# One gathered tile in 88 fetched row by row by SyncE, and segment tables fetched with one transfer a run: a graph network on one Trainium2 core

## The chip, the cores and the metric

The kernel runs on one core of one Trainium2 chip. The metric is device time in microseconds (us). The engines are named as in the profile: PE (TensorE; PEld is its weight load), DVE (VectorE), ACT (ScalarE), POOL (GpSimd) and SP (SyncE). SP computes nothing here: it issues DMAs, each with the register work for its addresses. In the profile's rows, SPq, DVEq and POOLq are the sequencers of these engines.

## The reference, cut to what matters

A graph has N = 6250 nodes with 128 numbers each and 200000 edges (src, dst), sorted by dst; an edge has 4 numbers of its own. Two convolutions and one attention run over the edges.

```python
def mesh_conv(x, src, dst, ea, w1, b1, g, bt, w2, b2):
    m = concatenate([x[dst], x[src], ea]) @ w1 + b1
    m = silu(group_norm(m, g, bt)) @ w2 + b2
    return segment_sum(m, dst) / clip(count(dst), 1)

h = silu(group_norm(mesh_conv(relu(layernorm(x)), ...))) + time_embedding
h = silu(group_norm(mesh_conv(h, ...))) + relu(layernorm(x))
q, k, v = (h @ w + b for each of three)
logits = (q[dst] * k[src]).sum(-1) * scale + (ea @ ew + eb)      # 8 heads
pe = exp(logits - segment_max(logits, dst)[dst])
o = segment_sum(pe / segment_sum(pe, dst)[dst] * v[src], dst) @ ow + ob
return x + h + group_norm(o)
```

The product with w1 is taken per node, not per edge: before each stage a table of x[dst]'s part (`a_d`) and one of x[src]'s part (`b_d`, in attention `kv_d`, 256 wide) lie in HBM, and what remains per edge is to fetch a row of each and add or multiply them.

## The kernel before

**Tiles.** The edges lie in 1563 tiles of 128, eight tiles to a chunk (TPC), 196 chunks (NCH). Three stages go over all chunks, one after another: conv 1, conv 2, attention. `pipeline` (L755) emits a stage; step n of its loop works on several chunks at once, and `in_order` (L743) pins the emitted order on DVE, SP, ACT and PE. So an instruction that waits holds all that is emitted behind it on its engine. A conv step emits:

- `fetch(n+2)`: SP loads the chunk's first row number into a register (`value`, L618) and fetches 112 rows of `a_d` into one of three buffers (`pk`, L647); for every second chunk it fetches the comparison tile `ohT` of two chunks (`load_group`: L631, 896 KB, and L634, 40 KB; two buffers). POOL gathers x[src]'s part: eight indirect DMAs, one a tile, 128 rows each (`gather`, L661), into one of four buffers g (in attention one of eleven).
- `products(n+1)`: PE multiplies pk and ohT to m (L1089, 8 products; in attention qe, L1294).
- `compared(n+2)`: ACT turns ohT into a one-hot matrix (L656, L657).
- `second`: for a chunk some steps back, DVE builds the one-hot `oh` (L667), norms h (L1111, L1114, L1115), ACT takes silu (L1116), PE sums by node (u, L1121), ACT and DVE put it into the node table.
- `first(n)`: DVE adds m and g into h (L1096), which frees the buffer of g; ACT squares it (L1098).
- `early`, `batch`, `aside`, `reduce`: a one-hot ahead of time, node work of finished windows, in conv 1 the preparation of tables for attention (`deferred`), and the variance (L1100).

The g buffer of a chunk comes free by L1096 of the chunk four before; POOL then gathers the next one or more chunks in one go. POOL's order isn't pinned, but POOL does hardly anything else.

**The attention's tables.** The maximum per segment is scanned over runs of up to eight chunks with two tables of marks, `nbs_d` and `nbe_d`. Both lie in HBM as one row of 128 per tile. A run needs them as [8 chunks x 8 heads, 1024], each chunk's row repeated for the eight heads, so `load_runs` (L1317) issues one DMA of 16 KB a chunk and table (L1323), which reads the row eight times: 392 in the stage, up to 16 in a row. `in_rows` (L468) writes these tables in conv 1, as part of `deferred`.

**Names of the waits.** "POOL g L661 <- DVE h L1096" is POOL's wait for a free buffer of g. "SPq L631 <- remote" and "SPq L647 <- remote" are SP's waits ahead of the fetches of ohT and pk, for a buffer that is still in use.

Of the kernel before, what the change touches and what calls it, by code (L numbers as in the profile page):

```python
# [8 lines left out]
FP = mybir.dt.float32  # L9
BF = mybir.dt.bfloat16  # L10
I32 = mybir.dt.int32
AF = mybir.ActivationFunctionType
# [3 lines left out]
SP = mybir.EngineType.SP  # L16
# [5 lines left out]
P = 128  # L22
D = 128
H = 8
# [3 lines left out]
TPC = 8  # L28
EPC = TPC * P
# [3 lines left out]
LG = 2  # L33
WN = 112
SOON = 24
TAILS = [7, 7, 6, 5, 4, 3, 4]
BY_ACT = 60
KE = 5
KW = WN + KE
DB = D + H  # L40
# [2 lines left out]
KV = 2 * D  # L43
EPS = 1e-5
BIG = 1e30
# [4 lines left out]
def kernel(ctx: ExitStack, tc: tile.TileContext, x, src, dst, eat, w, out):  # L50
# [9 lines left out]
    nc = tc.nc  # L60
    N = x.shape[0]
    EI = src.shape[1]
    NCH = -(-EI // TPC)
    EW = NCH * TPC
# [6 lines left out]
    dram = ctx.enter_context(tc.tile_pool(name="dram", bufs=1, space=DRAM))  # L71
# [8 lines left out]
    def by_chunk(t):  # L80
        return t.rearrange("p (c t) -> p c t", t=TPC)
# [8 lines left out]
    ident = const.tile([P, P], FP, name="ident")  # L90
# [53 lines left out]
    b_d = {i: dram.tile([NW * P, D], FP, name=f"b_d{i}") for i in (1, 2)}  # L144
    kv_d = dram.tile([NW * P, KV], FP, name="kv_d")
# [2 lines left out]
    dwl_d = dram.tile([P, EW], FP, name="dwl_d")  # L148
    dmod_d = dram.tile([P, EW], FP, name="dmod_d")
    rel_d = dram.tile([EW, P], FP, name="rel_d")  # L150
    nbs_d = dram.tile([EW, P], BF, name="nbs_d")
    nbe_d = dram.tile([EW, P], BF, name="nbe_d")

    dm0 = const.tile([P, EW], BF, name="dm0")
    ef = const.tile([P, EW], BF, name="ef")
# [39 lines left out]
    with tc.tile_pool(name="node0", bufs=1) as np_, tc.tile_pool(name="prep", bufs=1) as pp, \  # L195
# [8 lines left out]
        step = 8  # L204
# [38 lines left out]
        for a in range(0, NW, 4):  # L243
            m = min(4, NW - a)
# [12 lines left out]
            tp = pst.tile([P, 4, P], FP, name="tp")  # L257
# [96 lines left out]
    def steps_of(i):  # L354


        ends, due, n = {}, {}, 0
        for m in spread(i):
            ends[n + m] = list(range(n, n + m))
            due.setdefault(n + m + (n < NCH - (sum(TAILS) if i == 3 else SOON)), []).extend(ends[n + m])  # L360
            n += m
        waiting, todo, left = [], [], NCH
        while left:
            n = len(todo)
            waiting += due.get(n, ())
# [26 lines left out]
    def deferred(dp, ps):  # L392
# [56 lines left out]
        def bank():  # L449
            return ps.tile([P, 4, P], FP, name="nd", tag="nd")  # L450
# [16 lines left out]

        def in_rows(t, d_):  # L468

            for k in range(0, EW, 4 * P):  # L470
                yield from to_rows(t, d_, -BIG, bank(), dp.tile([P, 4, P], BF, name="sbd"), k, nc.sync)

        kept = []

# [147 lines left out]
    class Chunk:  # L622
        oh = None

    def load_group(c, pools):

        n = min(LG, NCH - c)
        m = min(n * TPC, EI - c * TPC)
        t = pools["ohT"].tile([P, LG, EPC], FP, name="ohT")
        f = t.rearrange("p c e -> p (c e)")  # L630
        nc.sync.dma_start(  # L631
            out=f[:WN, :m * P],
            in_=rel_d[c * TPC:c * TPC + m, :].rearrange("t p -> (t p)")[None, :].to_broadcast([WN, m * P]))
        nc.sync.dma_start(out=f[WN:KW, :m * P], in_=eat[:, c * EPC:c * EPC + m * P])  # L634
        pools[c // LG] = t
# [20 lines left out]
        nc.scalar.activation(k.ohT[:WN, :], k.ohT[:WN, :], AF.Square, bias=minus_p[:WN])  # L656
        nc.scalar.activation(k.ohT[:WN, :], k.ohT[:WN, :], AF.Relu, bias=1.0, scale=-4.0)  # L657

    def gather(k, g, table_d):
        for t in range(k.nt):  # L660
            nc.gpsimd.indirect_dma_start(  # L661
                out=g[:, t, :table_d.shape[1]], out_offset=None, in_=table_d,
                in_offset=bass.IndirectOffsetOnAxis(ap=k.src[:, t:t + 1], axis=0))
# [91 lines left out]
    def pipeline(i, stage, aside=iter(())):  # L755

        start = len(nc.cur_bb.bb.instructions)
        ends, todo = steps_of(i)
        starts = {n: j for j, (n, _) in enumerate(plans[i])}
        ahead = stage.ahead
        ks, under_way, said = {}, [], {}
        for c in range(ahead):
            ks[c] = stage.fetch(c)
            compared(ks[c])
        stage.products(ks[0])  # L770
        for n, seconds in enumerate(todo):
            if n + ahead < NCH:
                ks[n + ahead] = stage.fetch(n + ahead)
            if n + 1 < NCH and stage.soon:
                stage.products(ks[n + 1])
            run = [ks[c] for c in ends.get(n, ())]
            stage.root(run)
            if n + ahead < NCH and stage.soon:
                compared(ks[n + ahead])
            first = (lambda k: lambda: stage.first(k))(ks[n]) if n < NCH else None  # L780
            if stage.second(run, [ks.pop(c) for c in seconds], first) and first:
                first()
            stage.finish()
            if n + ahead < NCH and not stage.soon:
                compared(ks[n + ahead])
            if n + 1 < NCH and not stage.soon:
                stage.products(ks[n + 1])
            if n < NCH:
                stage.early(ks, n, todo[n + 1])
            if n in starts:  # L790
                for _ in aside:
                    pass
                under_way.append(stage.batch(starts[n]))
            for g in list(under_way):
                if said.get(g) == "held" and n + 1 in ends:
# [257 lines left out]
    def conv(i):  # L1053
# [4 lines left out]
        with ExitStack() as es:  # L1058
# [15 lines left out]
                nc.vector.tensor_copy(t, s)  # L1074
            np_, nd = pool("np", 1), pool("nd", 1, space=PSUM)
            nodes = Nodes(np_of(np_, "A", "o"), lambda: nd.tile([P, BN, D], FP, name="nd", tag="nd"))
            side = es.enter_context(ExitStack())
            aside = iter(())
            if i == 1:
# [53 lines left out]
            class Stage:  # L1133
                ahead, soon = 2, True
                sums, late, roots, next = [], [], False, 0
                var, j, sd = None, 0, None

                def fetch(self, c):
                    k = loads(c, pools, a_d[i], self.ahead)
                    k.g = gp.tile([P, TPC, D], FP, name="g")  # L1140
                    gather(k, k.g, b_d[i])
                    k.h = hs[c % len(hs)]
                    return k

# [68 lines left out]
                    add_late(self.sums[0])  # L1213

            stage = Stage()
            nodes.var = lambda: stage.var[:, NV:]
            pipeline(i, stage, aside)
            side.close()
# [43 lines left out]
    with ExitStack() as es:  # L1262
# [17 lines left out]
        def bank():  # L1280
            return banks()[:, 0, :].rearrange("p (t e) -> p t e", e=P)
# [35 lines left out]
        def load_runs(run, bp):  # L1317

            nb = {}
            for name, d_ in (("nbs", nbs_d), ("nbe", nbe_d)):  # L1320
                nb[name] = bp.tile([G * H, EPC], BF, name=name)
                for j, c in enumerate(run):
                    nc.sync.dma_start(  # L1323
                        out=nb[name][j * H:(j + 1) * H, :],
                        in_=d_[c * TPC:(c + 1) * TPC, :].rearrange("t p -> (t p)")[None, :].to_broadcast([H, EPC]))
            return nb

        def maxima(run, lg, nb, bp):
# [92 lines left out]
        class Stage:  # L1421
# [3 lines left out]

            def __init__(self, bp):
                self.bp = bp
                self.runs = list(steps_of(3)[0].values())
                self.nb = load_runs(self.runs.pop(0), bp)

            def fetch(self, c):
                k = loads(c, pools, a_d[3], self.ahead)
                k.g = gp.tile([P, TPC, KV], FP, name="g")
                gather(k, k.g, kv_d)
                return k

            def products(self, k):
# [79 lines left out]
                merge_late(self.sums[0])  # L1517
                add_late(self.sums[0])

        with tc.tile_pool(name="bpa", bufs=1) as bp, tc.tile_pool(name="ohTa", bufs=2) as pools["ohT"]:  # L1520
            pipeline(3, Stage(bp))

        n = NW - NWD
# [87 lines left out]
```

## Time and profile before

| what | value |
|---|---|
| median of 3 runs | 8112.13 us (8091.78 to 8127.0) |
| profiled execution, its own time | 8070.85 us |
| its span in the trace | 8068.5 us |
| granted PE clock, mean | 0.679 |
| instructions in the trace | 72388 |
| DMA engines, mean rate | 99 GB/s |

A row of a group reads: line, engine, operation, output<-inputs, count | busy us, mean ns of one | idle time before them, and what ended it. A row of a timeline reads: start, duration (of all in the row, if it says x16), engine, line, operation, and in brackets the idle time before it and what ended it; "issue" means that the engine waited for nothing that the profile shows. A row of the waits reads: engine and line, what it waited for, us in total, times, the longest. A row of one line's instructions reads: operation, count, duration in ns (shortest/median/longest), first and last start.

### The profile page before, as it was taken

To read this page: it belongs to the slowest core of one execution; us is meant where nothing else is said; L and a number is where in the kernel's file an instruction comes from. 1 tells how busy PE (TensorE), PEld (TensorE's weight loads), DVE (VectorE), ACT (ScalarE), POOL (GpSimd) and SP (SyncE) were. 2 spreads that over 40 slices of the span, in tenths; PEclk is the share of its full clock that TensorE was granted. 3 is DMA by queue.
4 is the path that set the end of the run, shared out by engine and by line. 5 is a ranking of instruction groups with operands and counts; after the bars stand their busy time and mean duration, and the time that the engine had idled before them with its cause. 6 is when DMAs were issued, how large, how long until landed. Compare 5 with 4: busy or idle time off the path is not lost. (4 is left out here: it accounts for less than half of the span.)

```text
span 8068.5 us, 72388 instructions
## 1 busy us (share of the span) xinstructions
PE 3978.0 (49%) x20935; PEld 3656.4 (45%) x20936; DVE 4993.0 (62%) x7274; ACT 3483.6 (43%) x5592; POOL 4485.6 (56%) x4706
## 2 busy tenths in 40 slices
PE   4555545544544454555555544344444555455444
PEld 3444444444443444444544544244444444444434
DVE  5767776666654566666777766255665655565446
ACT  4555555555544455555555544122222222234444
POOL 5666666666543666666566654455555555555541
PEclk7666666777666666666777767566666666666666
DMA  5433333333322333333333332343444444444431
GB/s 136 106 91 94 92 101 85 93 87 90 89 78 60 92 87 87 92 87 93 101 96 96 96 85 72 104 121 111 116 115 117 119 119 117 115 115 128 115 106 51
DMA packets 413975, 797.97 MB, mean 99 GB/s; under 512 B 102179, under 2 KB 274966, under 8 KB 379509
## 3 DMA queue, kind: packets, MB, share of 16 engines
q0 software_dynamic: 175056, 410.03, 19.0%
q1 hardware_dynamic: 232868, 379.58, 16.5%
q10 hardware_dynamic: 5632, 3.50, 0.2%
q8 instruction: 173, 2.83, 0.2%
q14 instruction: 246, 2.02, 0.1%
HBM read 751.77 MB, written 40.96 MB: 98 GB/s over the span
## 5 line engine op out<-in xcount | busy, mean ns | idle before, releaser
L661 POOL DMA_INDIRECT g<-b_d,src_i x3126 | 2969.5, 950 | 1917.1 <-DVE h L1096 987.6
L661 POOL DMA_INDIRECT g<-kv_d,src_i x1563 | 1490.2, 953 | 1363.6 <-DVE cm L1408 537.0
L1121 PE MATMUL u<-h,oh 128*128 128x129 f32 (+1 forms) x6252 | 1330.0, 381 | 1735.7 <-ACT h L1116 867.0
L1121 PEld LDWEIGHTS u<-h,oh 128*128 128x128 f32 x6252 | 1193.7, 284 | 1860.4 <-issue 943.9
L1089 PE MATMUL m<-pk,ohT 117*128 117x128 f32 x6252 | 1066.8, 324 | 687.1 <-issue 632.2
L1089 PEld LDWEIGHTS m<-pk,ohT 117*128 117x128 f32 x6252 | 988.1, 239 | 745.1 <-issue 696.5
L1372 PE MATMUL us<-v,oh 128*128 128x145 f32 x3126 | 740.0, 399 | 905.1 <-issue 549.2
L1372 PEld LDWEIGHTS us<-v,oh 128*128 128x128 f32 x3126 | 653.5, 282 | 975.9 <-issue 949.1
L1096 DVE TENSOR_TENSOR h<-m,g 128x1024 f32<-128x1024 f32 x392 | 475.1, 1212 | 971.9 <-remote 898.2
L1294 PE MATMUL qe<-pk,ohT 117*128 117x136 f32 x3126 | 588.6, 354 | 431.0 <-issue 247.0
L1294 PEld LDWEIGHTS qe<-pk,ohT 117*128 117x128 f32 x3126 | 548.7, 258 | 473.3 <-issue 286.2
L656 ACT ACTIVATE ohT<-ohT,minus_p 112x1024 f32<-112x1024 f32 x588 | 670.5, 1140 | 42.2 <-DMA ohT<-rel_d 29.6
L1116 ACT ACTIVATE h<-h 128x1024 f32<-128x1024 f32 x392 | 412.8, 1053 | 596.7 <-DVE h L1115 299.4
L657 ACT ACTIVATE ohT<-ohT 112x1024 f32<-112x1024 f32 x588 | 619.7, 1054 | 18.6
L1126 ACT ACTIVATE u<-u,mask 128x129 f32<-128x129 f32 (+1 forms) x784 | 263.8, 336 | 823.7 <-remote 763.7
L1100 DVE TENSOR_REDUCE var<-sq 128x64 f32<-128x1024 f32 x392 | 475.3, 1212 | 192.6 <-ACT sq L1098 85.2
L667 DVE TENSOR_TENSOR oh<-cps,dm 128x1024 f32<-128x1024 f32 x392 | 474.7, 1211 | 89.4 <-remote 79.2
L1385 ACT ACTIVATE us<-d 128x16 f32<-128x16 f32 x196 | 36.7, 187 | 1042.9 <-DVE d L1382 729.6
L1114 DVE TENSOR_TENSOR h<-h,cps 128x1024 f32<-128x1024 f32 x392 | 477.2, 1217 | 14.6 <-DVE h L1111 1.3
L1115 DVE TENSOR_TENSOR h<-h,cps 128x1024 f32<-128x1024 f32 x392 | 477.1, 1217 | 13.5 <-DVE h L1114 0.2
L1098 ACT ACTIVATE sq<-h 128x1024 f32<-128x1024 f32 x392 | 411.3, 1049 | 168.7 <-DVE h L1096 136.3
L1111 DVE TENSOR_TENSOR h<-h,cps 128x1024 f32<-128x1024 f32 x392 | 474.3, 1210 | 0.0
(286 smaller groups left out, 4387.7 us busy)
## 6 DMA issues: line engine op xcount, KB each, us to landing
ohT<-rel_d SPq DMA_DIRECT2D x291, 896.0 KB
g<-b_d,src_i POOLq DMA_INDIRECT x3126
pk<-a_d SPq DMA_DIRECT2D x588, 56.0 KB
g<-kv_d,src_i POOLq DMA_INDIRECT x1563
ohT<-in_eat_dram SPq DMA_DIRECT2D x291, 40.0 KB
a_d<-n_o SPq DMA_DIRECT2D x28, 256.0 KB
kv_d<-n_o SPq DMA_DIRECT2D x28, 256.0 KB
n_h<-h_d SPq DMA_DIRECT2D x19, 256.0 KB
```

What stands on the lines that cost most here:

```text
L656: nc.scalar.activation(k.ohT[:WN, :], k.ohT[:WN, :], AF.Square, bias=minus_p[:WN])
L657: nc.scalar.activation(k.ohT[:WN, :], k.ohT[:WN, :], AF.Relu, bias=1.0, scale=-4.0)
L661: nc.gpsimd.indirect_dma_start(out=g[:, t, :table_d.shape[1]], out_offset=None, in_=table_d, in_offset=bass.IndirectOffsetOnAxis(ap=k.src[ ...
L667: return nc.vector.tensor_tensor(k.oh[:, :k.nt, :], iota[:, None, :].to_broadcast([P, k.nt, P]), k.dm[:, :, None].to_broadcast([P, k.nt, P ...
L1089: nc.tensor.matmul(k.m[:, t, :], lhsT=lhs[:, t * P:(t + 1) * P], rhs=rhs, start=(j == 0), stop=(j == len(terms) - 1))
L1096: nc.vector.tensor_tensor(k.mt, k.m[:, :n], k.g[:, :n], ALU.add)
L1100: return lambda: nc.vector.tensor_reduce(var[:, at:at + n * H], sq[:, :n].rearrange("p t (g c) -> p (t g) c", c=HD), AX.X, ALU.add)
L1114: nc.vector.tensor_tensor(k.mt, k.mt, over_edges(gam, k.nt), ALU.mult)
L1115: nc.vector.tensor_tensor(k.mt, k.mt, over_edges(bet, k.nt), ALU.add)
L1121: nc.tensor.matmul(k.u[:, 0, :wide], lhsT=k.oh[:, t, :], rhs=k.h[:, t, :wide], start=(t == 0), stop=(t == k.nt - 1))
L1294: nc.tensor.matmul(k.qe[:, t // TB, at:at + DB], lhsT=lhs[:, t * P:(t + 1) * P], rhs=rhs, start=(j == 0), stop=(j == len(terms) - 1))
L1372: nc.tensor.matmul(k.u[:, :wide], lhsT=k.oh[:, t, :], rhs=k.v[:, t, :wide], start=(t == 0), stop=(t == k.nt - 1))
```

## The change

In each stage 17 chunks are picked (16, 27, ... 192: every 11th, `by_rows`). For these POOL gathers seven tiles, not eight. The eighth tile's 128 rows are fetched by SP into a tile of their own (`row_g`), in the 11 steps before the chunk's own fetch is due: in each step one instruction loads 12 row numbers into registers (8 in the last step), and then 12 DMAs fetch one row each (512 bytes, in attention 1 KB). There is such work in 187 of the 196 steps of each stage, 2176 row DMAs a stage. The row numbers come from a list on one partition (`row_at`, one DMA a picked chunk). In the step before the chunk is used, behind `early`, ACT copies `row_g` into the eighth tile of g (`put`). In SP's order a step's rows stand behind its pk and ohT, and ahead of those of the next step.

Each row is three instructions on SP (a register operation, a move, the DMA); SP's program grows from 4850 to 18135 instructions as built. The DMAs use eight completion semaphores in turn, so that a row waits for the DMA eight before it.

`nbs_d` and `nbe_d` are now [196, 8, 1024], with each chunk's row written eight times over, so that `load_runs` fetches a run with one DMA a table (some 56 in place of 392). They are written by four DMAs a table as before, with eight times the bytes, from transposes that take the tiles chunk by chunk (16 transposes a table, 13 before). The order on PE, DVE and ACT is otherwise as before; on POOL 51 gathers are missing.

```diff
+ROWS = 12
...
-    nbs_d = dram.tile([EW, P], BF, name="nbs_d")
-    nbe_d = dram.tile([EW, P], BF, name="nbe_d")
+    nbs_d = dram.tile([NCH, H, EPC], BF, name="nbs_d")
+    nbe_d = dram.tile([NCH, H, EPC], BF, name="nbe_d")
...
         def in_rows(t, d_):
-            for k in range(0, EW, 4 * P):
-                yield from to_rows(t, d_, -BIG, bank(), dp.tile([P, 4, P], BF, name="sbd"), k, nc.sync)
+            for c in range(0, NCH, P):
+                n = min(P, NCH - c)
+                for a in range(0, TPC, 4):
+                    tp = bank()
+                    for j in range(4):
+                        nc.tensor.transpose(tp[:n, j, :], by_chunk(t)[:, c:c + n, a + j], ident)
+                    yield
+                    sb = dp.tile([P, 4 * P], BF, name="sbd")
+                    nc.scalar.activation(sb[:n], tp[:n].rearrange("c t p -> c (t p)"), AF.Copy, scale=-BIG)
+                    yield
+                    nc.sync.dma_start(
+                        out=d_[c:c + n, :, a * P:(a + 4) * P], in_=sb[:n, None, :].to_broadcast([n, H, 4 * P]))
+                    yield
...
+    def by_rows():
+        span, first = -(-P // ROWS), LG + 3
+        return list(range(first + span, NCH - 1, span)), span
+
+    class Rows:
+        def __init__(self, pool, table_d, width):
+            self.pool, self.table_d, self.width = pool, table_d, width
+            self.chunks, self.span = by_rows()
+            self.starts = {c - 2 - self.span: c for c in self.chunks}
+            self.now, self.got = None, {}
+            self.at = {}
+            if self.chunks:
+                self.list_of(self.chunks[0])
+
+        def list_of(self, c):
+            t = self.pool.tile([1, P], I32, name="row_at")
+            col = c * TPC + TPC - 1
+            nc.sync.dma_start(out=t, in_=src[:, col:col + 1].rearrange("p o -> o p"))
+            self.at[c] = t
+
+        def step(self, n):
+            if n in self.starts:
+                c = self.starts[n]
+                self.now = [c, 0, self.pool.tile([P, self.width], FP, name="row_g")]
+                self.got[c] = self.now[2]
+                j = self.chunks.index(c) + 1
+                if j < len(self.chunks):
+                    self.list_of(self.chunks[j])
+            if self.now:
+                c, e, t = self.now
+                m = min(ROWS, P - e)
+                _, at = nc.values_load_multi_w_load_instructions(
+                    self.at[c][0:1, e:e + m], engines=[SP], min_val=0, max_val=N - 1,
+                    skip_runtime_bounds_check_because="a source node")
+                for j, a in enumerate(at):
+                    nc.sync.dma_start(out=t[e + j:e + j + 1, :], in_=self.table_d[bass.ds(a, 1), :self.width])
+                self.now[1] = e + m
+                if e + m == P:
+                    self.now = None
+
+        def put(self, k):
+            if k.c in self.got:
+                nc.scalar.copy(k.g[:, TPC - 1, :self.width], self.got.pop(k.c))
...
-    def gather(k, g, table_d):
-        for t in range(k.nt):
+    def gather(k, g, table_d, lone=()):
+        for t in range(k.nt - bool(lone and k.c in lone)):
...
             if n + ahead < NCH:
                 ks[n + ahead] = stage.fetch(n + ahead)
+            stage.rows.step(n)
...
                 stage.early(ks, n, todo[n + 1])
+            if n + 1 < NCH:
+                stage.rows.put(ks[n + 1])
...
-                for j, c in enumerate(run):
-                    nc.sync.dma_start(
-                        out=nb[name][j * H:(j + 1) * H, :],
-                        in_=d_[c * TPC:(c + 1) * TPC, :].rearrange("t p -> (t p)")[None, :].to_broadcast([H, EPC]))
+                nc.sync.dma_start(
+                    out=nb[name][:len(run) * H, :],
+                    in_=d_[run[0]:run[-1] + 1, :, :].rearrange("c h e -> (c h) e"))
```

Conv's and attention's `fetch` hand the picked chunks to `gather`; the row tiles have a pool of two buffers.

More of the change, by code (lines that the diff above doesn't have):

```diff
@@ L1076, in conv @@
             nodes = Nodes(np_of(np_, "A", "o"), lambda: nd.tile([P, BN, D], FP, name="nd", tag="nd"))
+            rw = pool("rw", 2)
             side = es.enter_context(ExitStack())
@@ L1140, in fetch @@
                     k.g = gp.tile([P, TPC, D], FP, name="g")
-                    gather(k, k.g, b_d[i])
+                    gather(k, k.g, b_d[i], self.rows.chunks)
                     k.h = hs[c % len(hs)]
@@ L1215, in conv @@
             stage = Stage()
+            stage.rows = Rows(rw, b_d[i], D)
             nodes.var = lambda: stage.var[:, NV:]
@@ L1427, in __init__ @@
                 self.bp = bp
+                self.rows = Rows(rw, kv_d, KV)
                 self.runs = list(steps_of(3)[0].values())
@@ L1433, in fetch @@
                 k.g = gp.tile([P, TPC, KV], FP, name="g")
-                gather(k, k.g, kv_d)
+                gather(k, k.g, kv_d, self.rows.chunks)
                 return k
@@ L1518, in flush @@
                 add_late(self.sums[0])
-        with tc.tile_pool(name="bpa", bufs=1) as bp, tc.tile_pool(name="ohTa", bufs=2) as pools["ohT"]:
+        with tc.tile_pool(name="bpa", bufs=1) as bp, tc.tile_pool(name="rwa", bufs=2) as rw, \
+                tc.tile_pool(name="ohTa", bufs=2) as pools["ohT"]:
             pipeline(3, Stage(bp))
```

## The prediction

> **What bounds the kernel now.** The chain of waits that ended last is no help: it holds no share above 0% and stays in the last microseconds. So the busy times come first, then the stretches by stage, then timelines of one stretch.
>
> ```profile
> PE 3978.0 (49%) x20935; PEld 3656.4 (45%) x20936; DVE 4993.0 (62%) x7274; ACT 3483.6 (43%) x5592; POOL 4485.6 (56%) x4706
> ...
> L661 POOL DMA_INDIRECT g<-b_d,src_i x3126 | 2969.5, 950 | 1917.1 <-DVE h L1096 987.6
> ```
> ```profile
> 0.00:2572.00 2572.00, 1286.64 (x7016) 1193.73 (x7018) 1680.97 (x1925) 1317.66 (x1635) 1496.10 (x1576) 0.70 0.34 92
> 2572.00:5090.00 2518.00, 1275.26 (x6994) 1183.30 (x6994) 1657.45 (x1738) 1282.87 (x1563) 1495.84 (x1567) 0.69 0.33 91
> 5090.00:8068.00 2978.00, 1416.08 (x6929) 1279.35 (x6928) 1654.58 (x3611) 883.03 (x2395) 1493.69 (x1564) 0.65 0.40 112
> ```
>
> No engine is full, in total or in a stage (the rows are conv 1, conv 2 and attention; the columns after the length are PE, weight load, DVE, ACT, POOL, clock, DMA share, GB/s). Several queues wait for each other in turn. What the turn looks like is seen in the timeline of POOL over five chunks of conv 2.
>
> ```profile
> 3288.66 0.95 POOL L661 DMA_INDIRECT g<-b_d,src_i  x1 [4.41 <-DVE h L1096]
> 3289.91 0.95 POOL L661 DMA_INDIRECT g<-b_d,src_i  x1 [0.30 <-issue]
> ...
> 3317.42 0.95 POOL L661 DMA_INDIRECT g<-b_d,src_i  x1 [0.30 <-issue]
> 3324.15 0.95 POOL L661 DMA_INDIRECT g<-b_d,src_i  x1 [5.78 <-DVE h L1096]
> ...
> 3348.21 0.95 POOL L661 DMA_INDIRECT g<-b_d,src_i  x1 [4.33 <-DVE h L1096]
> ```
>
> Gathers start every 1.25 us (3288.66 to 3289.91). There is a run of 24 (to 3318.37) and, from 3324.15, one of 16; between runs POOL waits some 5 us until DVE's `h` (L1096) frees a buffer of g. Five chunks take 59.55 us (3288.66 to 3348.21), **11.9 us a chunk**. L1096 needs PE's m, and PE's own timeline shows why it is late:
>
> ```profile
> 3304.34 2.26 PE L1121 MATMUL u<-h,oh 128*128 128x128 f32 x16 [3.04 <-ACT h L1116]
> 3309.13 0.27 PE L1089 MATMUL m<-pk,ohT 117*128 117x128 f32 x1 [2.54 <-issue]
> 3312.62 0.37 PE L1089 MATMUL m<-pk,ohT 117*128 117x128 f32 x1 [3.22 <-issue]
> ...
> 3320.33 4.16 PE L1089 MATMUL m<-pk,ohT 117*128 117x128 f32 x11 [0.34 <-issue]
> ```
>
> PE does sixteen products in 2 to 4 us; but late in POOL's run of 24 (18 us after its start) it issues one in 1.7 to 3.5 us, waiting for nothing shown, and goes on at speed 2 us after the run's end. **SP does the same**, which matters for this change. In attention a run's tables are fetched with 16 DMAs in a row (L1323); three such bursts, with the gathers near them:
>
> ```profile
> 5571.68 0.95 POOL L661 DMA_INDIRECT g<-kv_d,src_i  x1 [9.71 <-DVE cm L1408]
> ...
> 6038.94 0.94 POOL L661 DMA_INDIRECT g<-kv_d,src_i  x1 [10.58 <-DVE cm L1408]
> ...
> 6067.78 0.95 POOL L661 DMA_INDIRECT g<-kv_d,src_i  x1 [0.30 <-issue]
> ...
> 7561.86 0.95 POOL L661 DMA_INDIRECT g<-kv_d,src_i  x1 [0.30 <-issue]
> ```
> ```profile
> 5579.25 0.35 SPq L634 DMA_DIRECT2D ohT<-in_eat_dram  x1
> 5579.65 7.83 SPq L1323 DMA_DIRECT2D nbs<-nbs_d  x8
> 5587.58 9.49 SPq L1323 DMA_DIRECT2D nbe<-nbe_d  x8
> ...
> 6052.08 0.35 SPq L634 DMA_DIRECT2D ohT<-in_eat_dram  x1
> 6052.48 9.01 SPq L1323 DMA_DIRECT2D nbs<-nbs_d  x8
> 6063.59 9.10 SPq L1323 DMA_DIRECT2D nbe<-nbe_d  x8
> 6072.80 1.22 SPq L647 DMA_DIRECT2D pk<-a_d  x2
> ...
> 7568.39 2.31 SPq L1323 DMA_DIRECT2D nbs<-nbs_d  x7
> 7570.80 2.29 SPq L1323 DMA_DIRECT2D nbe<-nbe_d  x7
> ```
>
> The third burst falls after a run of eight that ended at 7562.8: 0.33 us a DMA. The second falls into a run of 24 (6038.94 to 6068.7): 20.2 us for 16, **1.26 us each**, and still slow until some 4 us after the run's end, where two pk fetches take 1.22 us in all. SP turns slow 8 us into the run in the first burst, 13 us in the second: I take 10.5 us. So a run of 24 (29.7 us) makes SP slow for 29.7 - 10.5 + 4 = 23.2 us, one of 16 (19.7 us) for 19.7 - 10.5 + 3 = 12.2 us (3 by choice, PE's 2 and SP's 4 being the ends), one of eight for none. Today this hurts SP little, as it is ahead of PE and waits for free buffers:
>
> ```profile
> SPq L631 <- remote: 2666.9, 151, 48.4
> SPq L647 <- remote: 1132.7, 92, 35.9
> ```
>
> That is 3800 us of waiting, which the change draws on.
>
> **The change, part by part.**
>
> *Rows by SP.* In 17 chunks of each stage the last tile isn't gathered: 51 of 4689 gathers go, 51 x 1.25 = 64 us of POOL, 42 of them in the convs. For each, SP issues 128 row fetches, 12 a step, in 187 of a stage's 196 steps: one register load of 12 values, and per row a register operation, a move and a DMA of one row. They stand behind pk and ohT of one step and **ahead of pk and ohT of the next**; PE's m, ACT's compare (L656) and everything behind them wait for those. The prices:
>
> ```profile
> L647 SPq FUSED_REGOPS  x588: 2/37/2097, 71.3 to 7969.9; - x196
> L647 SPq MOVE pk<-a_d x588: 2/29/1404, 71.5 to 7970.0; - x196
> L647 SPq DMA_DIRECT2D pk<-a_d x588: 2/322/1383, 71.6 to 7977.4; - x196
> ```
> ```profile
> L132 SPq DMA_DIRECT2D wcb<-in_c_b_dram x2: 248/249/250, 17.6 to 236.0; - x2
> ```
> ```profile
> L618 SPq TENSOR_LOAD <-lo_i x588: 3/468/1384, 70.7 to 7969.6; - x196
> L618 DVEq TENSOR_LOAD <-w_i x588: 298/304/929, 149.9 to 8041.4; - x196
> ```
>
> Medians: 0.037 + 0.029 + 0.25 (a [1x128] DMA) to 0.32 (pk's), and some 0.04 us between records (0.33 us a DMA in the fast burst, of which 0.29 busy): 0.43 to 0.51 us a row, I take 0.45, so 12 x 0.45 = 5.4 us a step. A load of 12 registers has no row: from one load's 0.47 to twelve of DVE's, 12 x 0.304 = 3.6; I take the middle, 2.0. What SP does already: load 0.47, pk 0.51, half of the pair for ohT 0.38, together 1.4. **SP needs 5.4 + 2.0 + 1.4 = 8.8 us a step at speed.** While SP crawls a row is three records of 1.26 us, 3.8 us, so work goes at 0.45/3.8, about an eighth.
>
> For a load of this kind the Trainium skill, "Runtime: NRT & Kernel Launch", Instruction fetch mechanics, gives about 200 ns a register even in bulk. By that rule twelve are an estimated 2.4 us, 0.4 above what I take, and the sum below would be some 150 us higher; the trace's 0.468 us for one register neither bears it out nor speaks against it for twelve.
>
> A chunk of conv has 11.9 us, and by the share of slow time five chunks hold 59.6 - 35.4 = 24.2 us at speed. SP needs 44 us at speed in them, and does an eighth of 35.4, 4.2 us of work, in the slow part. It is **15.6 us short in five chunks**; the two steps it is ahead are used up at once. The period then follows SP, by the pattern of POOL's runs. Each pattern's period is its slow time plus the work left for fast time:
> - 24 and 16 as now, 5 chunks: 35.4 + 44 - 4.2 = 75.2, 15.0 us a chunk.
> - runs of 16 (late chunks come in pairs, since ohT comes for two), 2 chunks: 12.2 + 17.6 - 1.5 = 28.3, 14.2.
> - 16 and 8, 3 chunks: 12.2 + 26.4 - 1.5 = 37.1, 12.4.
>
> I take the mean, 13.9 us, 1.95 above now, and keep 12.4 and 15.0 as ends. Two convs: 1.95 x 187 x 2 = **+729 us**, less the 42 us of gathers: **+687**. With a load of 0.47 us instead of 2.0 the middle pattern gives 12.6, with 3.6 us 15.8.
>
> In attention a chunk takes 2978/196 = 15.2 us, so eight take 121.5; runs such as 24, 24 and 16 make 58.6 of it slow, 63 fast. SP needs 8 x 8.8 + 1 for two table fetches = 71.4, less 58.6/8 = 7.3 done in the slow part, 64: about what there is. I cost it at **nothing**, cover being exactly these 63 us; should it be gone, one us of load more a step costs 187 us.
>
> *Tables of a run in one transfer.* 16 DMAs become two, a burst of 17 to 20 us in the slow part two records of 1.26. SP waits elsewhere in that stage, so this is room for the rows and no gain of its own. The tables are written eightfold in conv 1 (6.4 MB, at the stage's 92 GB/s some 70 us of transfer in a stage whose DMAs are 34% busy): hidden, at 0.
>
> *The copy.* ACT puts the fetched tile in place, 51 times, behind the last rows' arrival.
>
> ```profile
> L1364 ACT COPY v<-pe 128x64 f32<-128x64 f32 x196 | 50.8, 259 | 0.2
> ```
>
> Two to four times as wide, 0.3 to 0.4 us: under 20 us in an engine idle for half of each stage, at 0. As ACT is ordered, a copy whose rows are late holds the next compare; its rows are issued two steps earlier, so it adds nothing while SP itself is the last.
>
> Sum: 8070.85 + 687 = 8758, against the profiled execution, whose span is 8068.5. The median of the runs, 8112.13, lies 41 us above it, so I predict **8800**.
>
> **The rivals.**
> - *SP's slack swallows the rows.* For it: 3800 us of SP's waits; 374 steps x 7.4 us of new work is 2768. Then only gathers and bursts go: 8112 - 64 = 8048, to 7950 if the bursts were late for PE too. Against it: the waits lie in fast time alone, which must then be 44 of 59.6 us.
> - *POOL's runs fall apart to eights.* Late chunks could part all runs; then PE and SP are never slow, and SP's 8.8 us fit. POOL's 10 us and a wait of 1 give 11.0 us: -0.9 x 374 - 42 = -380, **7730**. It decides where a chunk is late by less than a run of 16 needs. Against it: ohT serves two chunks.
> - *The slow share stays* at 24 and 16: +3.1 x 374 = 1160, **9270**, more with a load above 2 us. For it: four g buffers allow long runs after any stall.
> - *The rows themselves prolong the crawl, or a row waits for a transfer eight before it,* ohT's above all. Price: 1 us a step is 374 us in the convs, 9170. The fast bursts (15 DMAs at 0.33 us) speak against the second.
>
> **How the numbers follow.** Forecast 0.64, slow share as now or longer (third and fourth) 0.20, slack 0.10, eights 0.06. The predicted time is the forecast's. Its own range is 12.4 to 15.0 us a chunk: +0.5 x 374 - 42 = 145 gives 8257, +3.1 gives 9230. Towards the unknown load (12.6 to 15.8 in the middle pattern, 1450 us at the upper end) I reach to 9400, and down to 8130, where the slack would have swallowed nearly all: what lies outside is the slack, the eights and a part of the third. Within 0.5%, about what a measurement of this kernel can tell from no change, lies a third of the slack case, 0.03; faster are the rest of it and the eights, 0.12; slower 0.85.
>
> **What would show it.** Right: SP's waits for free buffers shrink from 3800 us to under 1500; PE and ACT wait for pk and ohT; both conv stages grow by 300 us or more, attention by under 100; POOL's waits between its runs grow from 5 us to 8 or more; the load of 12 registers lies between 0.5 and 3.6 us. Wrong: conv stages unchanged with SP still waiting (the slack), or POOL in eights with PE's waits by issue gone (the eights). If attention grows as much as the convs, my share of slow time there is off.

## The result, and the profile after

The changed kernel takes 8814.33 us (median of 4, 8782.71 to 8839.5) where the kernel before takes 8111.1 us on the same chip (median of 4): ratio 1.0874, 95% interval 1.0839 to 1.0909, **8.7% slower**. Its profiled execution took 8839.5 us. **That holds for a chip on which SP and PE crawl while POOL gathers** (an instruction that waits for nothing shown then takes several times its usual time). **Two of the five groups of runs below fell on chips on which nothing crawls: there the kernel before takes 6230 us, and the change makes it 0.8% faster.** Each ratio is therefore against the kernel before on the same chip. Lengths of stages are compared with those of the one profile of the kernel before on a chip that crawls; its runs on such chips lie between 8022 and 8127 us, so they are good to some tens of us.

The page of the changed kernel, first the busy times, then the waits of all engines, in which PE and ACT now wait for what SP fetches (72388 instructions have become 92323, nearly all the new ones SP's):

```profile
span 8837.7 us, 92323 instructions
## 1 busy us (share of the span) xinstructions
PE 3931.5 (44%) x20941; PEld 3700.4 (42%) x20942; DVE 4997.2 (57%) x7274; ACT 3490.4 (39%) x5643; POOL 4428.7 (50%) x4655
```
```profile
POOL g L720 <- DVE h L1159: 1564.1, 264, 19.0
ACT ohT L715 <- DMA ohT<-rel_d: 1367.5, 180, 26.3
...
PE m L1152 <- DMA pk<-a_d: 661.3, 120, 16.2
```

ACT waits 1367.5 us for ohT (29.6 us before), PE 661.3 us for pk. L1159 is the old L1096, L720 the old L661: POOL's wait for a free g in the convs grew by 576 us, from 172 waits to 264. SP's own waits for free buffers, 3800 us before, are nearly gone (L690 fetches ohT, L706 pk, L675 a row):

```profile
SPq L690 <- remote: 211.9, 8, 44.5
SPq L675 <- DMA ohT<-rel_d: 71.9, 77, 3.3
SPq L706 <- remote: 64.9, 10, 33.6
SPq L675 <- DMA row_g<-b_d: 47.5, 98, 1.3
```

By stage (same columns as before; PE, PEld, DVE, ACT, POOL busy, clock, DMA share, GB/s), conv 1 is 276 us longer, conv 2 274, attention 219. The engines have no more to do than before (PE's weight loads are busy 44 us more, DVE and ACT 4 and 7, PE and POOL less); they wait more.

```profile
0.00:2848.00 2848.00, 1277.33 (x7017) 1207.43 (x7019) 1683.17 (x1925) 1316.90 (x1651) 1477.36 (x1559) 0.68 0.33 85
2848.00:5640.00 2792.00, 1271.80 (x6991) 1202.44 (x6992) 1661.27 (x1738) 1283.28 (x1581) 1477.44 (x1549) 0.68 0.31 82
5640.00:8837.00 3197.00, 1382.39 (x6936) 1290.52 (x6935) 1652.78 (x3611) 890.18 (x2412) 1473.87 (x1548) 0.66 0.37 104
```

The mechanism is seen in 55 us of conv 2: POOL's first gather of each run, SP's issues, and PE.

```profile
4001.52 0.94 POOL L720 DMA_INDIRECT g<-b_d,src_i  x1 [6.13 <-DVE h L1159]
...
4026.02 0.94 POOL L720 DMA_INDIRECT g<-b_d,src_i  x1 [4.55 <-DVE h L1159]
...
4039.14 0.94 POOL L720 DMA_INDIRECT g<-b_d,src_i  x1 [3.42 <-DVE h L1159]
```
```profile
4003.77 16.40 SPq L675 DMA_DIRECT2D row_g<-b_d  x12
4024.37 0.01 SPq L706 DMA_DIRECT2D pk<-a_d  x1
4024.63 7.26 SPq L675 DMA_DIRECT2D row_g<-b_d  x12
4033.32 0.01 SPq L706 DMA_DIRECT2D pk<-a_d  x1
4034.73 0.70 SPq L690 DMA_DIRECT2D ohT<-rel_d  x1
4035.46 0.71 SPq L693 DMA_DIRECT2D ohT<-in_eat_dram  x1
4037.61 4.81 SPq L675 DMA_DIRECT2D row_g<-b_d  x12
...
4044.49 9.32 SPq L675 DMA_DIRECT2D row_g<-b_d  x12
```
```profile
4034.61 2.02 PE L1152 MATMUL m<-pk,ohT 117*128 117x128 f32 x16 [2.24 <-DMA pk<-a_d]
```

Twelve rows took 16.40 us in a run of 16 (4001.52 to 4021.5), 7.26 us from just ahead of a run of eight into its first 6 us, 4.81 us from the break after it into the first 3 us of the next run, and 9.32 us from late in that run into the break after it. The pk behind the first twelve went out at 4024.37, the pk behind the second at 4033.32; PE's products stood waiting for the second. Over the trace, the median twelve rows took 9.5 us.

### The profile page after: what moved, and what is told of

Same layout as the page of the kernel before. It is cut to its first block, busy times and chain, and to the rows that moved or that the text cites. A ratio compares the mean times of both kernels' runs of the same rounds, so it can differ in the third digit from the quotient of the medians.

```text
span 8837.7 us, 92323 instructions
## 1 busy us (share of the span) xinstructions
PE 3931.5 (44%) x20941; PEld 3700.4 (42%) x20942; DVE 4997.2 (57%) x7274; ACT 3490.4 (39%) x5643; POOL 4428.7 (50%) x4655
## 5 line engine op out<-in xcount | busy, mean ns | idle before, releaser
L720 POOL DMA_INDIRECT g<-b_d,src_i x3092 | 2933.3, 949 | 2504.6 <-DVE h L1159 1564.1
L720 POOL DMA_INDIRECT g<-kv_d,src_i x1546 | 1469.4, 950 | 1592.1 <-DVE cm L1471 1038.7
L1152 PE MATMUL m<-pk,ohT 117*128 117x128 f32 x6252 | 1156.4, 359 | 1547.2 <-DMA pk<-a_d 661.3
L1184 PE MATMUL u<-h,oh 128*128 128x129 f32 (+1 forms) x6252 | 1215.1, 372 | 1412.9 <-ACT h L1179 891.7
L1152 PEld LDWEIGHTS m<-pk,ohT 117*128 117x128 f32 x6252 | 1086.5, 269 | 1612.2 <-issue 1001.2
L1184 PEld LDWEIGHTS u<-h,oh 128*128 128x128 f32 x6252 | 1134.5, 280 | 1487.0 <-ACT h L1179 936.1
L715 ACT ACTIVATE ohT<-ohT,minus_p 112x1024 f32<-112x1024 f32 x588 | 672.7, 1144 | 1597.8 <-DMA ohT<-rel_d 1367.5
L1435 PE MATMUL us<-v,oh 128*128 128x145 f32 x3126 | 707.2, 403 | 655.7 <-DVE nm L1468 320.6
L1159 DVE TENSOR_TENSOR h<-m,g 128x1024 f32<-128x1024 f32 x392 | 475.0, 1212 | 761.9 <-remote 684.6
L1373 DVE TENSOR_TENSOR g<-qe,g 128x768 f32<-128x768 f32 (+1 forms) x391 | 252.1, 686 | 1069.9 <-remote 985.5
L1375 ACT COPY ebs<-qe 128x48 f32<-128x48 f32 (+1 forms) x391 | 53.5, 188 | 1242.8 <-DVE g L1373 1146.8
```

Of the source, the lines that this page charges most:

```text
L720: nc.gpsimd.indirect_dma_start(out=g[:, t, :table_d.shape[1]], out_offset=None, in_=table_d, in_offset=bass.IndirectOffsetOnAxis(ap=k.src[ ...
L1152: nc.tensor.matmul(k.m[:, t, :], lhsT=lhs[:, t * P:(t + 1) * P], rhs=rhs, start=(j == 0), stop=(j == len(terms) - 1))
L1159: nc.vector.tensor_tensor(k.mt, k.m[:, :n], k.g[:, :n], ALU.add)
L1184: nc.tensor.matmul(k.u[:, 0, :wide], lhsT=k.oh[:, t, :], rhs=k.h[:, t, :wide], start=(t == 0), stop=(t == k.nt - 1))
L1435: nc.tensor.matmul(k.u[:, :wide], lhsT=k.oh[:, t, :], rhs=k.v[:, t, :wide], start=(t == 0), stop=(t == k.nt - 1))
```

## The experiments

**1. The tables alone.** Run together with the next three, on a chip without the crawl.

```diff
-        return list(range(first + span, NCH - 1, span)), span
+        return [], span
```

> The tables' part alone: a run's segment tables come in one transfer each, no tile is fetched row by row, all 4689 gathers stay. Theory (SP's issue time is the cause, and SP has room in the kernel before): 8111 us within 0.5%, attention's stage no shorter than 2930 us, as the bursts of 16 transfers lay in SP's waiting time. Rival (the tables' part is a gain that the rows hide): under 8050 us, attention shorter by 60 us or more. Rival (the eightfold writes cost time in conv 1): conv 1 longer by 30 us or more.

Measured: 6233.88 us against 6230.15, ratio 1.0004 (0.9994 to 1.0013): **no effect on this chip**; my numbers were for the other kind. What I had not expected was the other time of the kernel before. In this trace POOL never waits to speak of and SP's crawl isn't there, with as many instructions on every engine, DVE, ACT and POOL as busy as before and PE 393 us less:

```profile
PE 3585.1 (58%) x20941; PEld 3413.5 (55%) x20942; DVE 4992.5 (80%) x7274; ACT 3466.0 (56%) x5592; POOL 4484.0 (72%) x4706
...
L720 POOL DMA_INDIRECT g<-b_d,src_i x3126 | 2968.8, 950 | 964.3 <-issue 904.7
```

A gather has the same 950 ns; idle between gathers is 964.3 us where it was 1917.1, and nearly all is the 0.3 us between two of them. 4689 x 1.25 = 5861 us of 6234: **here POOL's gathers set the pace** (in experiment 5, leaving out 51 gathers gains 51 us), and SP waits for buffers that PE uses. Of SP's register operations and moves none takes over 0.6 us (0 of 1465; on the chip of the prediction 187 of 1465, in the changed kernel there 1953 of 14521).

**2. The rows alone.** The tables' lines as before the change, everything else as after it.

> The rows' part alone, with the tables fetched by 16 transfers a run as before. Theory: SP is what the stages wait for, so that 27 bursts come back with 14 more transfers each at 0.3 to 1.26 us; 27 x 14 x 0.3 to 1.26 is 110 to 480 us, some of it in attention's spare time: 8850 to 9150 us, all of the rise against the changed kernel in attention. Rival (SP isn't what attention waits for): 8814 us within 0.5%. Rival (the eightfold writes of the tables cost conv 1): below 8780 us.

Measured: 6193.36 us, ratio 0.9940 (0.9923 to 0.9957). My numbers were for the other chip and say nothing here. On this one the rows alone gain 37 us. The changed kernel gains 50 in experiment 5, but the intervals of the two ratios overlap, so a gain by the tables isn't shown.

**3. Fixed rows**, and **4. six rows a step**; both again without the crawl. The fixed rows are not the rows that the edges need: this kernel leaves out which row is fetched.

```diff
-                _, at = nc.values_load_multi_w_load_instructions(...)
-                for j, a in enumerate(at):
-                    nc.sync.dma_start(out=t[e + j:e + j + 1, :], in_=self.table_d[bass.ds(a, 1), :self.width])
+                for j in range(m):
+                    a = (c * 37 + (e + j) * 47) % N
+                    nc.sync.dma_start(out=t[e + j:e + j + 1, :], in_=self.table_d[a:a + 1, :self.width])
```
```diff
-ROWS = 12
+ROWS = 6
```

> The same 6528 row transfers of the same size in the same places, but of fixed rows in place of the source nodes' rows: no load of 12 registers and no register operation and move ahead of each transfer, so one SP record a row in place of three. Theory (what counts is the number of records that SP has to issue): 12 x 0.28 + 1.4 = 4.8 us a step in place of 7.1, 24 us in five chunks, of which some 8 us are done while SP crawls: it fits in the 24 us that SP runs at speed; 8050 to 8250 us. Rival (the transfers themselves cost the time: their traffic, or the wait of each for the one eight before it): 8700 to 8850 us.

> Six rows a step in place of twelve, for every 22nd chunk: half the rows. Theory (a threshold: SP's room is used up first): 6 x 0.41 + 0.6 + 1.4 = 4.5 us a step, 22 us in five chunks, fits: 8050 to 8200 us. Rival (each row costs its share): half the loss, about 8460 us.

Measured: 6176.71 us, ratio 0.9915 (0.9899 to 0.9932), and 6207.49 us, 0.9963 (0.9949 to 0.9977). Neither tells the theories apart where SP has room in any case: the gain goes by gathers removed, 51 and 24.

**5. The changed kernel again, more rows, and no rows,** together on another chip without the crawl. The kernel before: 6231.59 us. In the fourth kernel SP fetches the lists of row numbers but no rows, and the copies take zeros.

```diff
-ROWS = 12
+ROWS = 24
```
```diff
-ROWS = 12
+ROWS = 16
```
```diff
+                self.none = self.pool.tile([P, self.width], FP, name="row_g")
+                nc.vector.memset(self.none, 0.0)
...
-                self.now = [c, 0, self.pool.tile([P, self.width], FP, name="row_g")]
-                self.got[c] = self.now[2]
+                self.got[c] = self.none
```

> The changed kernel as it is, once more. In the four runs above the kernel before took 6230 us in place of 8111, POOL's gathers followed each other 1.25 us apart for hundreds on end, and neither SP nor PE ever crawled. Theory (the change costs what it takes of SP's fast time, and that is short only where SP crawls): where the kernel before takes about 6230 us, 7.1 us a step fit into a period of 10.1 us and 51 gathers go, so 6160 to 6200 us, 0.5 to 1.1% faster; where it takes about 8111 us, 8814 again. Rival (the rows cost time in either condition): over 6230 us where the kernel before takes 6230.

> Twice the rows a step: 24, for every sixth chunk, 31 chunks a stage, 93 gathers less in all. Theory (SP's issue time against the period): 24 x 0.41 + 1.1 + 1.4 = 12.3 us a step. Where nothing crawls that is above the period of 10.1 us, so each of 2 x 186 conv steps and 186 attention steps takes 12.3 us: about 6230 + 558 x 2.2 = 7450 us, the range 6900 to 7600. Where SP crawls: over 10000 us. Rival (SP isn't what counts, each gather less is 1.25 us): 6230 - 116 = 6114 us.

> 16 rows a step, for every eighth chunk, 23 chunks a stage, 69 gathers less in all. Theory: 16 x 0.41 + 0.9 + 1.4 = 8.9 us a step, still under 10.1: where nothing crawls, 6230 less up to 86 us, 6140 to 6190, at or below the changed kernel; where SP crawls, 9200 to 9700 us. Rival (rows cost in proportion): above the changed kernel in both conditions.

> The 51 tiles are neither gathered nor fetched row by row: zeros stand for their rows (that part of the work is left out); the copies, the lists of row numbers and the new tables stay. It is the most that taking 51 gathers off POOL can bring. Theory: where nothing crawls 6230 - 64 = 6166 us, within 15 us, as POOL's gathers set the pace; where SP crawls 8047 to 8111 us. Rival (POOL doesn't set the pace): 6230 us within 0.3%.

| rows a step | gathers gone | median us | ratio, 95% |
|---|---|---|---|
| 12, the changed kernel | 51 | 6181.32 | 0.9922 (0.9906 to 0.9939) |
| none, zeros copied | 51 | 6180.44 | 0.9921 (0.9905 to 0.9938) |
| 16 | 69 | 6615.69 | 1.0624 (1.0606 to 1.0642) |
| 24 | 93 | 7802.55 | 1.2528 (1.2507 to 1.2549) |

**Twelve rows a step cost nothing at all** here: within the intervals, the time is that of leaving them out. 16 rows cost 384 us: a threshold, as the theory has it, but lower than I had put it. 24 rows missed the range of 6900 to 7600 us by 200. SP's timeline with 16 rows a step, in conv 2:

```profile
3002.83 6.44 SPq L675 DMA_DIRECT2D row_g<-b_d  x16
3010.10 0.32 SPq L706 DMA_DIRECT2D pk<-a_d  x1
3010.53 0.37 SPq L690 DMA_DIRECT2D ohT<-rel_d  x1
3010.94 0.35 SPq L693 DMA_DIRECT2D ohT<-in_eat_dram  x1
3012.72 9.49 SPq L675 DMA_DIRECT2D row_g<-b_d  x16
3022.97 0.32 SPq L706 DMA_DIRECT2D pk<-a_d  x1
3024.50 6.43 SPq L675 DMA_DIRECT2D row_g<-b_d  x16
3031.76 0.32 SPq L706 DMA_DIRECT2D pk<-a_d  x1
```

SP hardly rests. Sixteen rows take 6.44 us (0.40 each); behind an ohT they take 9.49, since a row waits for the transfer eight before it, and for some of them that is ohT (452.8 us of such waits in this kernel, 270 times). My forecast had left this out. Two steps take 3031.76 - 3010.10 = 21.7 us, 10.8 a chunk, above POOL's 8 x 1.25 = 10.0. By that rate 552 steps cost 458 us, and 6231.59 - 86 + 458 = 6604 us is close to the time measured. In the changed kernel that wait is there too, but SP has the time:

```profile
SPq L675 <- DMA ohT<-rel_d: 515.2, 280, 5.9
SPq L690 <- PE m L1152: 399.4, 107, 12.6
SPq L690 <- PE qe L1358: 263.0, 52, 16.2
```

**6. Three buffers of g in place of four,** in the kernel before. This and the rest fell on chips that crawl; here the kernel before takes 8063.03 us.

```diff
-    gp_conv = gpc.enter_context(tc.tile_pool(name="gpc", bufs=4))
+    gp_conv = gpc.enter_context(tc.tile_pool(name="gpc", bufs=3))
```

> The kernel before with three buffers of g in the convs in place of four: POOL can run two chunks ahead, not three. Theory where SP and PE crawl late in long runs of gathers: with runs cut to 16 and 8 the crawl shrinks, so the convs take no longer for it in spite of the lost buffer, 7900 to 8250 us, PE's waits by issue in conv less than two thirds of before. Rival there (the buffer itself counts): over 8300 us. Where nothing crawls: POOL's gathers have no room for waits, 6230 to 6500 us.

Measured: 8033.52 us, ratio 0.9963 (0.9948 to 0.9978). In range, but it tests nothing: conv 2 still has 55 runs of 16 and 23 of 24 gathers (50 and 27 before, counting a break of over 0.5 us as a run's end), and PE's waits by issue in the convs, forecast at under two thirds, are as they were (1529 us; 1493 before).

**7. Fixed rows where SP crawls,** the kernel of experiment 3, with the kernel before at 8058.55 us.

> The fixed rows once more, hoped for where SP crawls (the kernel before near 8100 us): 12 row transfers a step of fixed rows, one SP record a row, no register load. Theory (the records that SP issues are the cost): at speed 11.1 rows a step on average at 0.28 us and some 4.1 us of other work make 7.2 us a chunk, at a fifth of the speed in slow time: 36 us in five chunks less 8 done in slow time, 28 against 24 us at speed: nearly fits, 8100 to 8350 us. Rival (the transfers, or their waits for the transfer eight before): 8650 to 8850 us. Where nothing crawls: 6177 us as measured.

Measured: 8081.69 us, ratio **1.0033** (1.0012 to 1.0053), 18 us under the theory's range. The same 6528 transfers, of the same size and at the same places, cost 0.3% in place of 8.7%. By stage, the convs are no longer than before (2560 and 2504 us; 2572 and 2518); attention is 70 us longer, in a profiled execution that was the slowest of eight (8114.86 us):

```profile
0.00:2560.00 2560.00, 1293.41 (x7033) 1200.14 (x7035) 1681.04 (x1928) 1320.50 (x1652) 1478.11 (x1559) 0.70 0.35 95
2560.00:5064.00 2504.00, 1290.40 (x6972) 1197.41 (x6970) 1657.47 (x1736) 1285.63 (x1579) 1472.75 (x1548) 0.69 0.35 91
5064.00:8112.00 3048.00, 1403.94 (x6939) 1286.79 (x6939) 1652.90 (x3611) 886.89 (x2412) 1474.89 (x1549) 0.66 0.39 109
```

SP still waits 987 us ahead of ohT for free buffers, and in the convs ACT waits 33.4 us for ohT and PE 1.5 us for pk, where the changed kernel has 1268.1 and 661.3. **It is the records that SP issues** (its instructions, as the trace lists them), **not the transfers,** that cost the time: 12 a step do not show, 37 do. The 25 that go are the load of 12 registers and the rows' register operations and moves; which of these counts most isn't parted, nor is the effect of fixed addresses in the DMAs that stay.

**8. Breaks in POOL's runs,** in the kernel before.

```diff
+    pause = const.tile([P, 512], FP, name="pause")
...
     def gather(k, g, table_d):
+        for _ in range(5):
+            nc.gpsimd.memset(pause, 0.0)
         for t in range(k.nt):
```

> The kernel before, with five memsets of a scratch tile on POOL ahead of each chunk's eight gathers, about 2.7 us that compute nothing. Theory (SP and PE crawl because POOL issues gathers without a break for longer than 8 to 13 us): where they crawl the memsets part all runs into eights, PE's waits by issue in the convs fall to less than a third, and with 588 chunks at 10.0 + 2.7 us the kernel takes 7500 to 7900 us, faster than without them. Rival (the crawl has another cause, the gathers' number or their transfers in flight): no change in the waits by issue, 8100 to 8500 us. Where nothing crawls: 588 x 12.7 + 125, some 7600 us.

Measured: 8859.72 us, ratio 1.0986 (1.0962 to 1.1011); my time was wrong. POOL's order isn't pinned, and the memsets came some ten at a time (5.8 us) ahead of eight gathers in the first half of conv 2 (to 4507 us), and not at all in the rest of it. That makes a comparison within one kernel. PE's waits in 300 us with breaks (3500 to 3800), then in 300 us without (4700 to 5000):

```profile
PE m L1092 <- DVE h L1099: 87.9, 19, 7.8
PE u L1124 <- ACT h L1119: 54.7, 15, 3.9
PE u L1124 <- issue: 14.7, 4, 3.9
```
```profile
PE u L1124 <- issue: 62.5, 41, 5.1
PE u L1124 <- ACT h L1119: 58.5, 11, 14.1
PE m L1092 <- issue: 22.9, 17, 3.1
```

With eights parted by 5.8 us PE hardly waits by issue: 14.7 us against 85.4. **On this chip the crawl goes with POOL's long runs.** Gathers are also fewer in the stretch with breaks (152 against 190 in the 300 us), so whether the length of a run or the number of transfers in flight counts isn't parted. A chunk takes some 15.6 us with the breaks, which cost more than the crawl.

**9. Rows in the convs alone,** with the kernel before at 8118.5 us.

```diff
                 self.rows = Rows(rw, kv_d, KV)
+                self.rows.chunks, self.rows.starts = [], {}
```

> The changed kernel with the rows in the convs alone: attention gathers all its tiles on POOL, and has the new tables in one transfer a run. Where SP crawls (the kernel before near 8080 us): theory (the rows cost attention its rise, the tables cost it nothing): attention as before, 2843 us within 40, each conv 275 us longer, in all 8580 to 8680 us. Rival (the tables' transfers themselves cost attention): attention 60 us or more longer than before. Where nothing crawls: 34 gathers less, 6230 - 43 = 6187, within 12 us.

Measured: 8563.3 us, ratio 1.0533 (1.0487 to 1.0579), 17 us under the theory's range. (Its "2843 us" for attention is a slip: the kernel before has 2978, and the range is worked out from that.) The profiled execution took 8618.78 us, the slowest of four; by stage 253, 262 and 33 us above the kernel before's:

```profile
0.00:2825.00 2825.00, 1268.48 (x7016) 1200.42 (x7017) 1683.00 (x1925) 1316.39 (x1650) 1480.72 (x1558) 0.69 0.33 86
2825.00:5605.00 2780.00, 1265.34 (x6987) 1194.65 (x6987) 1661.02 (x1739) 1283.66 (x1582) 1482.74 (x1548) 0.68 0.31 82
5605.00:8616.00 3011.00, 1441.96 (x6939) 1307.09 (x6939) 1653.71 (x3611) 882.92 (x2395) 1495.22 (x1566) 0.65 0.41 111
```

So with the tables alone attention is 33 us longer in this execution, and 186 of the changed kernel's 219 us go with the rows. By the medians the rows in attention cost 703 - 445 = 258 us: some 190 to 260 us, which one profile of each can't tell more closely.

## Why the prediction was right, and where it wasn't

The forecast was 8800, the time 8814, and the cause was the one named: SP late by its own issuing. That the number is so near is luck, as three errors cancel. The convs were put 137 us too high (687 for 550), attention 219 too low (nothing for 219), and 41 us were added for the median, where the profiled execution now lay 25 above it.

Of the signs that were to show the forecast right, SP's waits, the waits for pk and ohT and the load of 12 registers came as said. Three did not: the convs grew by 276 and 274 us, not by 300 or more; attention by 219, not under 100; and POOL's wait for a free g didn't become longer (5.7 us each before, 5.9 after) but more frequent, 264 times for 172.

- **SP late, by its own issuing: shown.** SP's waits for free buffers fell from 3800 to 277 us (I had said under 1500), PE and ACT wait for pk and ohT, and with one record a row in place of three and no load of registers the cost is gone, and those waits with it (experiment 7). The rival of the transfers falls with it.
- **The price of a row at speed, 0.45 us: nearly right,** 4.81/12 = 0.40, where no row waits for an ohT.
- **The load of 12 registers, 2.0 us: mis-sized.** This row of the changed kernel has a median of 0.756 us; 16 registers take 1.173 us, 24 take 1.633 (experiment 5), 0.06 to 0.07 us a register. That is a third of the 0.2 us that the Trainium skill's page, "Runtime: NRT & Kernel Launch", Instruction fetch mechanics, gives; the page speaks of registers loaded from HBM, where these come from a tile in SBUF.

```profile
L671 SPq TENSOR_LOAD <-row_at x561: 3/756/2098, 120.2 to 8703.9; - x187
```

- **A row while SP crawls, 3.8 us, and no crawl in runs of eight: both wrong,** in opposite directions. Twelve rows in a run of 16 took 16.40 us, 1.37 a row: its three records do not each take 1.26 us, as I had them do. Around runs of eight twelve rows took 7.26 and 9.32 us, which the forecast had at 12 x 0.45 = 5.4. Taking all runs of seven gathers or more that follow a break of 3 us, 381 of the 2096 DMAs, moves and register operations of SP that start 4 to 6 us into a run take over 0.6 us in the changed kernel, and 2 of 223 in the kernel before; 16 to 18 us into a run 207 of 237 and 40 of 60; from 3 to 4 us after its end 4 of 1476 and 4 of 194. So the crawl follows the runs, and it sets in earlier where SP issues more: the rival that the rows prolong it came true in part.
- **The rise of 1.95 us a chunk: too large.** The period after the change is as forecast (between the 200th and the 1400th gather of conv 2, 13.8 us a chunk for 13.9), but the same stretch takes 12.2 us before, not the 11.9 of the five chunks that I took. The convs grew by 550 us in place of 687. POOL's runs were cut shorter than in any of my patterns: conv 2 has 92 of eight or seven, 47 of 16 or 15 and one of 24, where it had 8, 50 and 27 (two odd ones at its ends aside). So the runs did fall apart to eights for the most part, without the gain of that rival, as SP crawls in eights too.
- **Attention at nothing: the step that failed.** It grew by 219 us, 186 of them the rows'. I set 64 us of work against "about what there is", 63, worked out from an assumed mix of runs, and called that no cost. After the change PE and ACT wait in attention, too, for what SP fetches, 252 us in all:

```profile
ACT ohT L715 <- DMA ohT<-rel_d: 99.3, 29, 11.6
PE qe L1358 <- DMA pk<-a_d: 83.0, 13, 15.8
PE qe L1358 <- DMA row_g<-kv_d: 70.0, 6, 13.3
```

Of such waits there are none in this stage before, and 4.8 us with the rows in the convs alone (experiment 9). SP's own waits in attention, which the prediction doesn't show, were 835.6 + 253.0 us for ohT and pk before, and some 680 us more in rows that name PE; 187 steps of 7.4 us are 1384. So in sum there was room, but no reserve in it: my reading, which no run tests by itself, is that what SP is late varies from chunk to chunk and is paid each time.
- **"The fast bursts speak against" a wait for the transfer eight before: wrong.** The ohT ahead of the burst that I quoted had been issued 6.7 us earlier; with 16 rows a step the first follows it by 2.2 us (3010.53 to 3012.72). On the crawling chip SP's rows waited some 72 us in all for it, on the other 515.
- **The slack that swallows the rows** had 0.10. It is what happens where nothing crawls, as the time is that of leaving the rows out, within the intervals. Against it I had the crawl, which was right for the chip that the trace was from. (By the single chances faster adds up to 0.13 and slower to 0.84, where I gave 0.12 and 0.85, and the 9270 of the third rival leaves out the 42 us of gathers.)

What stays open is why SP and PE crawl on some chips and not on others (one that crawls was met in two groups and crawled in both; each of the others was met once). The kernel, the gathers' 950 ns and their spacing of 1.25 us are the same. POOL's queue moved 175056 packets in 19.0% of 16 engines' 8068.5 us in the one (0.140 us each) and in 26.8% of 6233.8 us in the other (0.153 us), so its transfers were no slower under the crawl. That fetches of instructions are delayed would fit the steps of 0.7 us, but the packets of the two instruction queues took no longer either: 1.12 and 0.46 us each under the crawl (q8, q14), 1.16 and 0.47 without.

The traces differ in one more thing. On the chips that crawl many updates of semaphores are missing from the trace, and PE's come late. For the kernel before, 3729 of DVE's 5801 updates are there, and 499 of PE's 1383 stand more than 3 us behind the last PE instruction that could have made them; in experiment 1 it is 5792 of 5802, and 2 of 1521. So a wait ended by "remote" is there one whose releaser the trace doesn't show; DVE's such waits for m and qe end at updates of PE's semaphore. Whether the recording of the trace has a part in the crawl no run here tells.

Nothing here is shown to be best on both kinds of chip. Without the crawl the changed kernel itself, at 0.992, is as good as leaving the gathers out; with it the kernel before with three buffers of g, at 0.996, is the best here, and that was not run without the crawl.

## What to carry to other kernels

Work moved to an engine that only issues is paid in records, and the room for it has to be summed stage by stage, with the waits of that stage and not of the whole span: where nothing crawled, 12 rows a step were free and 16 cost 6%; where SP crawled, 12 cost 8.7%. Where rows of a trace show an engine at two speeds, ask what turns the second on, since a kernel tuned under one may answer a change with the other sign. A burst of small transfers behind a large one on the same eight semaphores waits for the large one.

## What the runs showed of the hardware that I had not expected

- The same kernel takes 6230 us on two chips and 8059 to 8118 us on others. A gather takes 950 ns on both, DVE's and ACT's operations are the same to 0.3% (1212 and 1140 ns for `h` and `ohT`), PE's product m 324 ns in place of 312. What differs is SP and PE during POOL's runs, where a record of SP can take 0.7 or 1.4 us in place of 0.03 to 0.3.
- A load of many registers on SP takes 0.06 to 0.07 us a register (0.756 us for 12, 1.633 for 24).
- With 24 rows a step and no crawl, the granted PE clock is 0.687, with 12 it is 0.772: a clock as low as in the crawling executions (0.675) also comes where nothing crawls and PE waits for SP (1077.8 us for pk).
